# Cross-attention with layer norm: score matmuls of 32 x 128 split into tiles of 32 x 64

## The chip, the cores and the metric

The kernel runs on one core of a Trainium2 chip. The core has a matrix engine (TensorE, PE in the profile, with its weight loads shown as PEld), a vector engine (VectorE, DVE), an activation engine (ScalarE, ACT), a general engine (GpSimd, POOL) and a queue that issues most DMAs (SyncE, SP). The metric is the device time of one execution in microseconds (us). The kernel before took 534.93 us, the median of three runs (534.4 to 535.43).

## The reference

Cross-attention of 4 x 2048 query rows on 4 x 77 context rows, 512 columns, 16 heads of 32 columns, then a residual and a layer norm, in float32:

```python
qs  = (q @ wq).reshape(4, 2048, 16, 32).transpose(0, 2, 1, 3)
ks_ = (k @ wk).reshape(4, 77, 16, 32).transpose(0, 2, 1, 3)
vs  = (v @ wv).reshape(4, 77, 16, 32).transpose(0, 2, 1, 3)
scores = einsum('bhqd,bhkd->bhqk', qs, ks_) / sqrt(32)
scores = where(mask, -inf, scores)
attn = einsum('bhqk,bhkd->bhqd', softmax(scores), vs)
out = attn.transpose(0, 2, 1, 3).reshape(4, 2048, 512) @ wo + q
out = (out - mean(out)) / sqrt(var(out) + 1e-5) * gamma + beta
```

Here `q` is `x`, and `k` and `v` are both the context. The change touches only the product of `qs` and `ks_`.

## The kernel before, in words

**Tiles.** The 8192 query rows are 64 tiles t of 128 rows; 16 tiles belong to one batch and share its 77 keys, its values and its mask. Two tiles make a pair. Heads come in four groups g of four (j = 0 to 3): head 4g + j has its 32 columns in partitions 32j to 32j + 31 of the transposed query projection `q` (512 rows wide, `qd` in the code) and of the transposed keys `kct`.

**Work of one tile, by engine.**
- `q_visit` (matmuls L160, 12 for 512 query rows and one m): query projection on PE from split operands (`xth`, `xtl`, `wqh`, `wql`); DVE copies it out (`q_evac`, L177).
- `scores` (L273 to L290, matmul L283): for each g and j one matmul. The loaded operand is `q` for one head (32 partitions, 128 query rows as columns), the streamed operand is `kct` (32 partitions, 77 keys), the result is 128 x 77 in a PSUM bank. Bank `sc[j]` holds the four heads of one j side by side. So a matmul uses 32 of the array's 128 rows and all 128 columns, and four of them, with j = 0 to 3, use four different row groups and write four different banks.
- `maxima` (L297, DVE): per head, adds the mask, moves the scores to SBUF (`pbuf`) and takes the row's maximum (`nm`).
- `exps` (L311, ACT): per head exponential and row sum. `recip` (L322, DVE) and `normalise` (L327, POOL) divide.
- `transp` (L351, DVE) transposes in blocks of 32, and `regroup` (DMAs L363, 12 a pair, on SP) sorts the blocks into `PT`.
- `av` (matmul L381, in the very last tiles `av_tile`, L396): attention times values for a pair. The loaded operand has 96 partitions and 32 columns; four heads use four column groups side by side. ACT and DVE take the result out in two halves (`AH` L412, `AL` L416).
- `o_proj` (matmul L445, 12 a tile): output projection from `AH`, `AL`, `woh`, `wol`. In the end some tiles also get their residual through PE (`resid`, L434). Then `residual` (L454) and the moments on DVE, the scaling on ACT, gamma and beta on POOL, and the store.

**Order.** Every engine runs its instructions in the order in which the code issues them. All PSUM results share eight banks in turn (`bank`, eight buffers), so a matmul group waits until the bank that it gets has been read. The first 54 tiles (27 pairs, `CUT`) are issued by a loop; in its regular part PE's order for a pair u, u + 1 is scores(u), o_proj(u - 6), one q_visit, scores(u + 1), av of the pair two before, o_proj(u - 5), one q_visit. Once in a batch DVE also builds the next batch's mask (`mask_bias` L264 and L265, `mask_nan` L269 to L271), in two consecutive pairs. The last ten tiles are issued from the text `ORDER`, in which an `S54` is scores(54), and so on. Before the loop come the loads, the splitting of the weights, the keys and the first query projections.

Of the kernel before, what the change touches and what calls it, by code (L numbers as in the profile page):

```python
# [17 lines left out]
P = 128  # L18
D = 512
H = 16  # L20
HD = 32
NK = 77
# [4 lines left out]
GH = 4  # L27
# [40 lines left out]
def xattn_layernorm(  # L68
# [15 lines left out]
    nc = tc.nc  # L84
    NB = mask.shape[0]
    TPB = mask.shape[2]
# [8 lines left out]
    def bank(name):  # L95
        return ps.tile([P, 512], F32, tag="mm", name=name)
# [8 lines left out]
    kct = const.tile([P, NG, NB, NK2], F32, name="kct")  # L105
# [28 lines left out]
    def keys_of(h):  # L134
        return slice(TAIL_K, NK2) if h % 2 == 0 else slice(0, NK)
# [137 lines left out]

    def scores(t):
        qs = qd[t // 4]
        rs = slice((t % 4) * P, (t % 4) * P + P)
        nmax[t] = sb.tile([P, H], F32, tag="nm", bufs=3, name=f"nm_{t}")
        sums[t] = sb.tile([P, H], F32, tag="sum", bufs=3, name=f"sum_{t}")
        sc = scs[t] = [bank(f"sc_{t}_{j}") for j in range(GH)]
        for g in range(NG):  # L280
            for j in range(GH):
                q = slice(HD * j, HD * (j + 1))
                nc.tensor.matmul(  # L283
                    sc[j][:, g * NK : (g + 1) * NK],
                    qs[q, g, rs],
                    kct[q, g, t // TPB, keys_of(j)],
                    start=True,
                    stop=True,
                )

    def maxima(t, lo, hi):
        pb = pbuf[t % NPB]
# [242 lines left out]
    for c in range(NC_D):  # L535
        split(x0h[:, c], x0l[:, c], f0[c // 2 * 2][:, 0, c % 2])
        split(wqh[:, c], wql[:, c], stage_a[:, 0, c])
        for m in range(NG):
            for n, (w, r) in enumerate(((wqh, x0h), (wqh, x0l), (wql, x0h))):
# [4 lines left out]
                    start=(c == 0 and n == 0),  # L544
                    stop=(c == NC_D - 1 and n == 2),
# [37 lines left out]
    for u in range(0, 2 * CUT, 2):  # L583
# [6 lines left out]
        for t in (u - 4, u - 3):  # L590
            if t >= 0:
                load_x(t)
        scores(u)
        maxima(u, 0, H // 2)
        for q in evac:
# [45 lines left out]
        if k == TPB - 2 and m + 1 < NB:  # L641
            mask_nan(m + 1)

        scores(u + 1)
        maxima(u + 1, 0, 3 * H // 4)
        recip(u)
# [42 lines left out]

    tile_ops = {  # L690
        "S": scores, "r": recip, "n": normalise, "t": transp, "W": av_tile, "x": load_x, "X": resid, "O": o_proj,
        "+": residual, "u": rsqrt_one, "y": centre, "z": finish, "k": scale, "f": affine, "w": store,
    }
# [81 lines left out]
```

## Time and profile before

| | us |
|---|---|
| Time, median of three runs | 534.93 |
| The profiled execution: span of its instructions | 533.1 |
| PE busy | 522.3 (98%) |
| PE weight loads busy (beside PE) | 399.1 (75%) |
| DVE busy | 486.2 (91%) |
| ACT busy | 459.6 (86%) |
| POOL busy | 400.7 (75%) |
| L283 score matmuls, 2048 instructions, busy on PE | 72.5 |

The profiled execution has its own span, 533.1 us from the first to the last instruction; the runs' times are taken separately and hold a little more than that span. How to read the views: in the **timeline** a row is a start, a length, the engine, line, operation and tile, and a count (x32: 32 instructions merged); the length runs to the end of the last. A row of the **windows** is a stretch in us, its length, then busy us and count for each engine, the clock that PE was granted, the busy share of the DMA engines and GB/s. A row of a **line's instructions** is a count, then shortest, median and longest duration in ns and the first and last start. A row of the **groups by line** has busy us and mean ns of one, then the idle time before them and what ended it. The **chain that ended last** goes back from the last instruction to what released each step. Matmul ends are modelled: a matmul's duration holds its way through the array, so several overlap, and the rate is read from starts.

### The profile page before, as it was taken

What the parts mean: (1) busy time and instruction counts of PE and PEld (TensorE: products, weight loads), DVE (VectorE), ACT (ScalarE), POOL (GpSimd) and SP (SyncE); (2) the same over time, 40 slices, a digit from 0 to 9 for tenths busy, and PEclk for the clock granted to TensorE, in tenths of its full rate; (3) what the DMA queues carried; (4) which work ended last, traced back from release to release, by engine and by line L of the source; (5) the groups of instructions that cost most, each with busy time, mean ns of one, the idle gap of its engine ahead of it and who ended that gap; (6) DMA issues with size and microseconds to landing.
All of it is one profiled execution on the core that took longest, in us unless ns stands there. A gap on an engine that the chain in (4) does not pass through costs nothing.

```text
span 533.1 us, 16107 instructions
## 1 busy us (share of the span) xinstructions
PE 522.3 (98%) x4810; PEld 399.1 (75%) x4810; DVE 486.2 (91%) x2592; ACT 459.6 (86%) x2215; POOL 400.7 (75%) x363
## 2 busy tenths in 40 slices
PE   8999999999999999999999999999999999999994
PEld 6977777777777777777777777777777777776672
DVE  5689989999998889889998998889999989999897
ACT  6687799999899999998899999998899999998600
POOL 0626547998798988887899888888799888665751
PEclk9999999999999999999999999999999999999997
DMA  8934667788677887787677787867687775849744
GB/s 300 402 120 111 202 173 195 222 232 226 176 187 213 227 215 208 208 226 201 179 213 214 208 221 217 232 165 211 191 216 216 219 191 159 219 129 281 226 138 157
DMA packets 58695, 109.96 MB, mean 206 GB/s; under 512 B 9392, under 2 KB 11056, under 8 KB 58608
## 3 DMA queue, kind: packets, MB, share of 16 engines
q1 hardware_dynamic: 55424, 102.64, 68.6%
q0 software_dynamic: 2304, 5.24, 3.5%
q10 hardware_dynamic: 880, 1.05, 0.7%
q8 instruction: 38, 0.62, 0.5%
q14 instruction: 49, 0.40, 0.2%
HBM read 41.79 MB, written 16.78 MB: 110 GB/s over the span
## 4 chain that ended last, share of the span: by engine, by line
PE 88%; DMA 5%; DVE 4%; issue 1%; SPq 1%; ACT 0%; DVEq 0%
PE pq L160 32%; PE po L445 30%; PE sc L283 12%; PE pa L381 9%; DMA PT<-B 2%; PE pv L221 2%; DMA out<-o 2%; PE pk L186 1%; DVE B L351 1%; DVE pbuf L297 1%; DMA stage_a<-wq 1%; PE pq L540 1%; DVE o_end L504 1%; DVE o_end L501 1%; SPq L363 0%
## 5 line engine op out<-in xcount | busy, mean ns | idle before, releaser
L311 ACT ACTIVATE pbuf<-pbuf,nm 128x77 f32<-128x77 f32 x1024 | 352.9, 352 | 31.4 <-DVE nm L297 26.5
L311 ACT ACTIVATION_READ_ACCUMULATOR pbuf<-pbuf,nm 128x1 f32 x1024 | 197.3, 193 | 0.0
L327 POOL TENSOR_TENSOR pbuf<-pbuf,ri 128x1232 f32<-128x1232 f32 x63 | 142.9, 2268 | 61.1 <-DVE ri L322 47.4
L297 DVE CUSTOM_DVE_ANT_0 pbuf<-sc,mb 128x77 f32<-128x77 f32 x1024 | 169.0, 231 | 4.9 <-PE sc L283 3.3
L445 PE MATMUL po<-woh,AH 128*128 128x512 f32 x256 | 108.6, 424 | 0.0
L445 PE MATMUL po<-wol,AH 128*128 128x512 f32 x256 | 100.4, 392 | 0.0
L445 PE MATMUL po<-woh,AL 128*128 128x512 f32 x256 | 100.1, 391 | 0.0
L160 PE MATMUL pq<-xth,wqh 128*128 128x512 f32 (+1 forms) x256 | 98.4, 385 | 0.0
L160 PE MATMUL pq<-xtl,wqh 128*128 128x512 f32 (+1 forms) x256 | 97.9, 382 | 0.0
L160 PE MATMUL pq<-xth,wql 128*128 128x512 f32 (+1 forms) x256 | 97.8, 382 | 0.0
L351 DVE STREAM_TRANSPOSE B<-pbuf 128x1280 f32<-128x1280 f32 x64 | 95.5, 1493 | 1.9 <-POOL pbuf L327 1.8
L297 DVE DVE_READ_ACCUMULATOR2_ANT nm<- 128x1 f32 x1024 | 84.0, 82 | 0.0
L283 PEld LDWEIGHTS sc<-kct,q 32*128 32x128 f32 x2048 | 63.0, 186 | 22.6 <-issue 12.0
L283 PE MATMUL sc<-kct,q 32*128 32x77 f32 x2048 | 72.5, 277 | 0.0
L153 POOL TENSOR_TENSOR xtl<-xtf,xth 128x1024 fp32r<-128x1024 f32 x28 | 67.1, 2397 | 1.9 <-ACT xth L149 1.9
L482 POOL TENSOR_TENSOR o<-o,bet 128x512 f32<-128x512 f32 x48 | 63.1, 1314 | 3.8
L445 PEld LDWEIGHTS po<-woh,AH 128*128 128x128 f32 x256 | 48.0, 187 | 23.1 <-DVE nm L297 6.6
L481 POOL TENSOR_TENSOR o<-o,gam 128x512 f32<-128x512 f32 x48 | 61.6, 1284 | 0.2
L381 PE MATMUL pa<-PT,vsb 96*32 96x256 f32 x992 | 60.0, 382 | 1.6 <-DMA out<-o 0.9
L445 PEld LDWEIGHTS po<-woh,AL 128*128 128x128 f32 x256 | 48.1, 188 | 10.7
L160 PEld LDWEIGHTS pq<-xth,wqh 128*128 128x128 f32 x256 | 48.1, 188 | 10.2 <-DVE nm L297 0.4
L445 PEld LDWEIGHTS po<-wol,AH 128*128 128x128 f32 x256 | 48.1, 188 | 9.6 <-issue 1.4
(106 smaller groups left out, 664.4 us busy)
## 6 DMA issues: line engine op xcount, KB each, us to landing
PT<-B SPq DMA_DIRECT2D x346, 128.0 KB, 2.4
xtf<-xT SPq DMA_DIRECT2D x28, 512.0 KB, 4.8
o<-x SPq DMA_DIRECT2D x56, 256.0 KB, 4.9
out<-o SPq DMA_DIRECT2D x56, 256.0 KB, 2.9
PT<-B POOLq DMA_DIRECT2D x21, 128.0 KB, 5.2
o_end<-x SPq DMA_DIRECT2D x8, 256.0 KB, 5.4
out<-o_end SPq DMA_DIRECT2D x8, 256.0 KB, 2.4
xtf<-xT SPq DMA_DIRECT2D x4, 256.0 KB, 5.0
```

What stands on the lines that cost most here:

```text
L153: nc.gpsimd.tensor_tensor(l, fx.pop((g, c)), h.bitcast(F32), ALU.subtract)
L160: nc.tensor.matmul(pq, w[:, c, m * P : (m + 1) * P], r[:, c, rs], start=(n == 0), stop=(n == 11))
L221: nc.tensor.matmul(pv[:NK2, :], ctx_s[c][i][:, b, :], v[c], start=(n == 0), stop=(n == 11))
L283: nc.tensor.matmul(sc[j][:, g * NK : (g + 1) * NK], qs[q, g, rs], kct[q, g, t // TPB, keys_of(j)], start=True, stop=True,)
L297: nc.vector.tensor_tensor_reduce(pb[:, h // 2, (h % 2) * NK : (h % 2 + 1) * NK], scs[t][j][:, g * NK : (g + 1) * NK], mb[:, t % TPB, keys_ ...
L311: nc.scalar.activation(pb[:, h // 2, (h % 2) * NK : (h % 2 + 1) * NK], pb[:, h // 2, (h % 2) * NK : (h % 2 + 1) * NK], AF.Exp, bias=nmax[t ...
L327: nc.gpsimd.tensor_tensor(pv, pv, rv.to_broadcast((P, NP, 2, NK)), ALU.mult)
L351: nc.vector.transpose(bt.rearrange("p c q r -> p q c r"), pbuf[t % NPB].rearrange("p q (c r) -> p q c r", c=5),)
L381: nc.tensor.matmul(pas[b, g // 2][HD * j : HD * (j + 1), (g % 2) * BLK : (g % 2 + 1) * BLK], vsb[:, 2 * b // TPB, HD * h : HD * (h + 1)], ...
L445: nc.tensor.matmul(pos[t], a[:, c, rs], w[:, c, :], start=(first and c == 0 and n == 0), stop=(c == NC_D - 1 and n == 2),)
L481: nc.gpsimd.tensor_tensor(o, o, gam, ALU.mult)
L482: nc.gpsimd.tensor_tensor(o, o, bet, ALU.add)
```

## The change: what it does

`scores` issues two matmuls where it issued one: the first for query rows 0 to 63 of the tile, the second for rows 64 to 127. Each loads 32 partitions x 64 columns of `q` and streams the same 77 columns of `kct`; the results go to partitions 0 to 63 and 64 to 127 of the same bank and columns as before. In the array the second half takes columns 64 to 127, so that with four row groups eight tiles of 32 x 64 lie side by side. The order is: for each g first the four j of the first half, then the four j of the second. All that reads the scores is unchanged.

```diff
     def scores(t):
         qs = qd[t // 4]
-        rs = slice((t % 4) * P, (t % 4) * P + P)
...
         for g in range(NG):
-            for j in range(GH):
-                q = slice(HD * j, HD * (j + 1))
-                nc.tensor.matmul(
-                    sc[j][:, g * NK : (g + 1) * NK],
-                    qs[q, g, rs],
-                    kct[q, g, t // TPB, keys_of(j)],
-                    start=True,
-                    stop=True,
-                )
+            for half in range(0, P, P // 2):
+                for j in range(GH):
+                    q = slice(HD * j, HD * (j + 1))
+                    r0 = (t % 4) * P + half
+                    nc.tensor.matmul(
+                        sc[j][half : half + P // 2, g * NK : (g + 1) * NK],
+                        qs[q, g, r0 : r0 + P // 2],
+                        kct[q, g, t // TPB, keys_of(j)],
+                        start=True,
+                        stop=True,
+                    )
```

## The prediction

> **What bounds the kernel now.** I read the page first (busy shares, then the chain that ended last), then the windows by stage, and last the timeline of TensorE (PE) around single stages.
>
> ```profile
> PE 522.3 (98%) x4810; PEld 399.1 (75%) x4810; DVE 486.2 (91%) x2592; ACT 459.6 (86%) x2215; POOL 400.7 (75%) x363
> PE 88%; DMA 5%; DVE 4%; issue 1%; SPq 1%; ACT 0%; DVEq 0%
> PE pq L160 32%; PE po L445 30%; PE sc L283 12%; PE pa L381 9%; DMA PT<-B 2%; PE pv L221 2%; DMA out<-o 2%; PE pk L186 1%; DVE B L351 1%; DVE pbuf L297 1%; DMA stage_a<-wq 1%; PE pq L540 1%; DVE o_end L504 1%; DVE o_end L501 1%; SPq L363 0%
> L454 DVE TENSOR_TENSOR o<-po,o 128x512 f32<-128x512 f32 x53 | 36.3, 686 | 17.2 <-PE po L445 17.1
> ```
>
> PE is the bound: 98% busy, 88% of the last chain, and the longest wait of VectorE (DVE) is for PE, 17.1 us at the residual. The score stage, L283, is 12% of the chain. How near are the others? The windows hold busy us and instruction counts of PE, PE's weight loads (PEld), DVE, ScalarE (ACT) and GpSimd (POOL).
>
> ```profile
> 20.00:80.02 60.02, 60.02 (x543) 46.71 (x541) 52.51 (x308) 48.75 (x249) 30.66 (x16) 1.00 0.61 179
> 80.02:202.64 122.62, 122.62 (x1154) 94.06 (x1153) 114.89 (x631) 118.05 (x571) 106.43 (x89) 1.00 0.78 210
> 202.64:325.25 122.61, 122.61 (x1154) 94.05 (x1153) 112.95 (x630) 115.12 (x553) 105.77 (x88) 1.00 0.77 208
> 325.25:432.57 107.32, 107.32 (x1010) 82.30 (x1009) 99.43 (x552) 100.60 (x484) 92.61 (x77) 1.00 0.77 209
> 432.57:490.00 57.43, 57.43 (x606) 42.17 (x606) 56.65 (x361) 52.29 (x282) 41.14 (x43) 1.00 0.69 187
> ```
>
> From 20 to 432.57 us PE has no idle time. That is the regular loop (two query tiles, one pair, in 122.61/8 = 15.33 us). ACT is close behind (115.12 of 122.61 in eight pairs), DVE next (112.95). From 432.57 on, in the hand-ordered end, DVE is busy 56.65 of 57.43 us.
>
> **The change part by part.** It replaces 16 matmuls of a tile by 32 of half the columns. First, what one stage consists of.
>
> ```profile
> 202.32 0.39 PE L160 MATMUL pq<-xth,wql 128*128 128x512 f32 x1
> 202.64 1.13 PE L283 MATMUL sc<-kct,q 32*128 32x77 f32 x32
> 203.70 0.50 PE L445 MATMUL po<-woh,AH 128*128 128x512 f32 x1
> ...
> 202.63 0.98 PEld L283 LDWEIGHTS sc<-kct,q 32*128 32x128 f32 x32 [0.35 <-issue]
> ...
> 202.63:202.66 0.03, 0.02 (x4) 0.03 (x4) 1.00 0.40 68
> 202.66:202.74 0.08, 0.08 (x4) 0.08 (x4) 1.00 1.32 282
> 202.74:202.80 0.06, 0.06 (x4) 0.06 (x8) 1.00 0.64 137
> ...
> L283 PEld LDWEIGHTS sc<-kct,q x2048: 181/187/187, 22.1 to 485.0; 32*128 32x128 f32 x187
> L283 PE MATMUL sc<-kct,q x2048: 270/270/330, 22.1 to 485.0; 32*128 32x77 f32 x187
> ...
> 202.71 1.06 PE sc L283 x32
> ```
>
> 64 tiles x 16 matmuls are 1024, the profile has 2048: an f32 matmul is two instructions (two passes), each with its own load. The windows show four loads and four matmuls started together, then nothing, then the next four loads: rounds of four, one per group of 32 rows, eight rounds a stage. The length of a round, from the block of 1.13 us: 1.13 less the last matmul's 0.27, less the 0.06 by which the first is longer (330 against 270 ns), less 0.02 for the spread of four, over 7 = 0.111 us. The loads, 0.98 less 0.187 less 0.02 over 7, give 0.110: the next four come when the previous four are through. A stage takes 1.06 us to the next stage's first matmul: 0.86 of rounds and 0.20 of emptying the array.
>
> What sets the 0.111? The attention matmuls (pa) have four column groups side by side, with short loads:
>
> ```profile
> 210.40 1.93 PE L381 MATMUL pa<-PT,vsb 96*32 96x256 f32 x32
> ...
> 515.90 1.96 PE L396 MATMUL pa<-PT,vsb 96*32 96x128 f32 x64
> ...
> L381 PEld LDWEIGHTS pa<-PT,vsb x992: 106/110/110, 59.7 to 503.4; 96*32 96x32 f32 x199
> L381 PE MATMUL pa<-PT,vsb x992: 376/379/403, 59.7 to 503.6; 96*32 96x256 f32 x199
> ...
> L396 PE MATMUL pa<-PT,vsb x64: 272/273/297, 515.9 to 517.6; 96*32 96x128 f32 x64
> ...
> 210.40 0.42 PE L381 MATMUL pa<-PT,vsb 96*32 96x256 f32 x4
> ...
> 210.40 0.14 PEld L381 LDWEIGHTS pa<-PT,vsb 96*32 96x32 f32 x5
> ```
>
> By the same reckoning a round with 256 moving columns is (1.93 - 0.379 - 0.024 - 0.02)/7 = 0.215 us, one with 128 is (1.96 - 0.273 - 0.024 - 0.02)/15 = 0.1095: 0.83 ns a column, so 77 columns would need 0.067 us. The score round takes 0.111, so its 128-column load is what it waits for, not the 77 columns that stream.
>
> After the change a load has 64 columns. Estimate of its time: half of 0.111 is 0.056; by the two load durations (187 ns for 128 columns, 110 for 32: 0.80 ns a column) it is 0.111 - 64 x 0.8 = 0.060. Issuing: four matmuls with their loads start within 0.42 - 0.403 = 0.02 us, 6 to 7 ns each, so eight take 0.053. All of it lies under the 0.067 of streaming. **If the eight tiles run at once**, a round has eight matmuls and lasts 0.067, and a stage still has eight rounds. Its length: 0.04 for the longer first matmul (between the 24 ns of pa and the 60 of sc), 7 x 0.067 = 0.47, 7 x 0.0067 = 0.05 for the spread, 0.20 of emptying: 0.76 us against 1.06. **0.30 us saved a stage.** The bounds of the unknown part: a round no shorter than the 0.053 of issue (0.40 saved), no longer than two turns of 0.067 (0.18 lost; below).
>
> Nothing else moves: the same order on every engine, the same four banks, no DMA, no new wait, since only the last matmul of a bank is waited for and the second half's first writes come behind the first half's on the same engine. PE issues 128 instructions a stage where it issued 64; the 0.053 above is their price, and it stays hidden as long as streaming is longer.
>
> How much reaches the end? The stages S0 to S53 lie ahead of 432.57, where PE is without a gap: 54 x 0.30 = 16.2 us. Of the last ten I count nothing:
>
> ```profile
> 454.43 8.17 PE pq L160 x36
> 466.65 1.42 DVE B L351
> 469.46 3.86 DMA out<-o
> 474.04 1.42 DVE B L351
> ```
>
> there the chain passes to DVE and its transposes, and DVE is full in the window. What is late next in the loop: eight pairs would take 122.61 - 16 x 0.30 = 117.8 us. ACT needs 115.12 in one window, but 118.05 in the first, so 0.3 is lost there. And ACT is made to wait, in two bursts a batch, when DVE does the mask work:
>
> ```profile
> L311 ACT ACTIVATE pbuf<-pbuf,nm 128x77 f32<-128x77 f32 x256 | 88.3, 354 | 7.5 <-DVE nm L297 7.5
> ```
>
> These 7.5 us are its whole slack in eight pairs; 2.7 would be left, so it catches up more slowly, the AH copies come later, and the output projection may wait for them. I take 0.4 us for each of three batches, and 1.2 us of ACT and DVE still late when the end begins, where DVE cannot make it up. Both are judged, between nothing and half of the gain. Sum: 16.2 - 0.3 - 1.2 - 1.2 = 13.5 us. The profiled span is 533.1, so 519.6; the median of the runs, 534.93, stands 1.8 above that span, so **521.4 us**.
>
> A rule of the Trainium skill speaks against the change: "TensorE: Matmul & The Clock Gate", The mechanism, says that a weight load overlaps matmuls in flight only where they use another row group. The two halves share their row group. By it a round would be a load and a matmul one after the other. The trace disagrees as far as it goes: in the row at 210.40 five loads lie in 0.14 us, the fifth beside four matmuls of 0.4 us on the same 96 rows. The same page measured 16 tiles of 32 by 32 at 10.6 times one tile's rate; no run here shows rows and columns split at once.
>
> **The rivals.**
>
> (1) The halves take turns (slower). In this trace row groups run side by side (sc) and column groups do (pa), never both. If the two halves of a row group stream in turn, a round is 2 x 0.067 = 0.134 against 0.111: 8 x 0.023 = 0.18 us a stage, and as PE is the bound all of 54 stages count: +9.9, **544.8**; with all 64, 546.7. It decides once a round passes 0.111, that is when less than 0.023 of 0.067 overlaps. Against it: four column groups take their own streams from the same rows at full rate in pa.
>
> (2) Loads wait for the matmuls of their row group (slower): a round of 0.060 + 0.067 = 0.127, +0.13 a stage, 54 stages: +6.9, **541.8**. The page named above states this. The 210.40 row speaks against it.
>
> (3) Matmuls start strictly in the code's order, so that the second pass of the first half holds up the second half: a group of heads then takes 2 x (0.067 + 4 x 0.0067) = 0.188 instead of 2 x 0.111, 4 x 0.034 = 0.14 a stage, 54 stages: -7.3, **527.6**. Against it: now four first passes start within 0.03 us, with their second passes later, so a pass that waits doesn't hold up other tiles.
>
> (4) No gain: the loads of the two halves share one path, 2 x 0.056 = 0.111 a round as now, **534.9**. The five overlapping pa loads speak against it.
>
> **How the numbers follow.** Forecast 0.62, (1) 0.13, (2) 0.05, (3) 0.13, (4) 0.07. The forecast's own range: all 64 stages at 0.30 give 534.9 - 19.2 = 515.7; with half of the gain lost between the engines, 526. To hold 8 in 10 the range must also take in (3) and (4): 515.5 to 536.0, which leaves out (1) and (2), 0.18. A measurement of this kernel tells about 0.2% (1.07 us) from no change. Faster: the forecast and (3), 0.75. Same: (4), 0.07. Slower: (1) and (2), 0.18.
>
> **What would show it.** L283 in the timeline: 64 matmuls of 32x77 in a block of about 0.83 us (0.56 to the last start and 0.27), eight starting together; 1.1 or less than 0.6 would refute the round of 0.067. The next stage 0.76 us after the first score matmul. The pair at 14.7 us in the windows, PE still without idle time; if ACT or DVE is full there and PE waits at L445, the loss between engines is larger than I took. The end, from S54 on, as long as before, about 100 us. It is wrong if rounds are longer than 0.111, or if the shorter stage only adds idle time before L445.

## The result and the profile after

The changed kernel takes **533.93 us** (median of 20 runs, 532.62 to 536.01); before, measured beside it, 535.12 (20 runs). The ratio is 0.9979, 95% interval 0.9970 to 0.9989: about 1.2 us faster, where 13.5 were forecast. The profiled span is 531.8 us, before 533.1.

The page of the changed kernel, busy times, chain and groups (most line numbers have moved by one):

```profile
PE 514.6 (97%) x6858; PEld 393.0 (74%) x6858; DVE 485.3 (91%) x2592; ACT 459.4 (86%) x2215; POOL 401.1 (75%) x363
PE 29%; ACT 28%; DVE 26%; DMA 9%; issue 3%; SPq 3%; POOL 1%; DVEq 0%; ACTq 0%
L382 PE MATMUL pa<-PT,vsb 96*32 96x256 f32 x992 | 60.2, 381 | 7.5 <-DMA o<-x 1.9
L284 PE MATMUL sc<-kct,q 32*64 32x77 f32 x4096 | 62.5, 238 | 0.4 <-DVE vsb L228 0.4
```

The same group of pa in the page of before:

```profile
L381 PE MATMUL pa<-PT,vsb 96*32 96x256 f32 x992 | 60.0, 382 | 1.6 <-DMA out<-o 0.9
```

PE is 7.7 us less busy, but the span is only 1.3 shorter. Ahead of pa there are now 7.5 us of idle time, where there were 1.6. With such gaps on PE the chain no longer stays on it: from 88% it falls to 29%. That does not make ACT and DVE the bound, as the windows of the same eight pairs show:

```profile
80.83:202.75 121.92, 120.27 (x1666) 92.61 (x1665) 114.43 (x631) 118.04 (x571) 106.51 (x89) 1.00 0.80 212
202.75:324.62 121.87, 120.25 (x1665) 92.63 (x1664) 112.55 (x630) 114.90 (x553) 105.92 (x88) 1.00 0.79 209
431.33:490.00 58.67, 57.45 (x930) 41.94 (x930) 57.66 (x361) 54.18 (x291) 41.83 (x45) 1.00 0.72 189
```

Eight pairs take 121.9 us against 122.6, and PE is idle for 1.6 of them, 0.2 a pair; in the end DVE is full, as before. Where is PE idle? The timeline of PE around an even and an odd score stage, and the same odd stage in the row of pa's instructions (PEldq: what PE's sequencer does ahead of a load), of the changed kernel:

```profile
202.75 0.95 PE L284 MATMUL sc<-kct,q 32*64 32x77 f32 x64
203.63 0.50 PE L446 MATMUL po<-woh,AH 128*128 128x512 f32 x1
...
209.27 0.95 PE L284 MATMUL sc<-kct,q 32*64 32x77 f32 x64
210.40 0.85 PE L382 MATMUL pa<-PT,vsb 96*32 96x256 f32 x12 [0.18 <-PE sc L284]
...
L382 PEldq EVENT_SEMAPHORE  x6: 51/51/51, 209.9 to 210.6; - x6
```

and the odd stage before:

```profile
209.34 1.13 PE L283 MATMUL sc<-kct,q 32*128 32x77 f32 x32
210.40 0.85 PE L381 MATMUL pa<-PT,vsb 96*32 96x256 f32 x12
...
L381 PEldq EVENT_SEMAPHORE  x4: 51/51/51, 209.6 to 210.0; - x4
```

The even stage has become 0.18 us shorter, 0.88 from its first matmul to po's. The odd one has become 0.07 longer, 1.13 to pa's. In the odd stage the sequencer takes pa's waits (eight DMA queues, DVE and PE, in five instructions ahead of the first load) one every 0.106 us. Before, there was no wait for PE among them, and the four instructions had been taken by 210.0, under the score matmuls; now the first comes at 209.9, and pa's load starts at 210.37, behind the fifth.

Inside a stage the timeline of its first part, matmuls and loads, shows what was forecast and what was not:

```profile
202.75 0.54 PE L284 MATMUL sc<-kct,q 32*64 32x77 f32 x33
...
202.75 0.39 PEld L284 LDWEIGHTS sc<-kct,q 32*64 32x64 f32 x33 [0.35 <-issue]
```

33 matmuls start within 0.54 - 0.22 = 0.32 us (the last one's own length taken off), in rounds of eight, which from the second on are 0.067 us apart: in the single instructions they begin at 202.865, .931, .998. That is the forecast round. The other 31 need 0.41: after the 33rd load, 0.253 us into the stage, one comes at 0.319 and the next at 0.374, and from there a whole f32 matmul (two loads, two passes) comes every 16.7 ns. The last starts 0.726 us after the first, not 0.557.

A pair's two stages thus give 0.18 - 0.07 = 0.11 us where 0.61 (twice 0.304) was forecast, and the pair takes 15.24 us (431.33 - 80.83 over 23) against 15.33.

### The profile page after: what moved, and what is told of

It is laid out like the page before. It is cut to its first block, busy times and chain, and to the rows that moved or that the text cites. A ratio compares the mean times of both kernels' runs of the same rounds, so it can differ in the third digit from the quotient of the medians.

```text
span 531.8 us, 20432 instructions
## 1 busy us (share of the span) xinstructions
PE 514.6 (97%) x6858; PEld 393.0 (74%) x6858; DVE 485.3 (91%) x2592; ACT 459.4 (86%) x2215; POOL 401.1 (75%) x363
## 4 chain that ended last, share of the span: by engine, by line
PE 29%; ACT 28%; DVE 26%; DMA 9%; issue 3%; SPq 3%; POOL 1%; DVEq 0%; ACTq 0%
ACT pbuf L312 23%; PE po L446 10%; PE pq L160 9%; DVE pbuf L298 7%; DVE B L352 5%; DMA PT<-B 4%; PE pa L382 3%; PE sc L284 3%; DVE q L177 3%; DMA o<-x 3%; ACT AH L413 3%; SPq L364 2%; DVE st L460 2%; ACT o L478 2%; PE pk L186 1%
## 5 line engine op out<-in xcount | busy, mean ns | idle before, releaser
L312 ACT ACTIVATION_READ_ACCUMULATOR pbuf<-pbuf,nm 128x1 f32 x1024 | 201.4, 197 | 0.0
L284 PEld LDWEIGHTS sc<-kct,q 32*64 32x64 f32 x4096 | 51.9, 130 | 23.6 <-issue 16.5
L284 PE MATMUL sc<-kct,q 32*64 32x77 f32 x4096 | 62.5, 238 | 0.4 <-DVE vsb L228 0.4
```

The lines of the kernel that those rows point to most:

```text
L284: nc.tensor.matmul(sc[j][half : half + P // 2, g * NK : (g + 1) * NK], qs[q, g, r0 : r0 + P // 2], kct[q, g, t // TPB, keys_of(j)], start= ...
L312: nc.scalar.activation(pb[:, h // 2, (h % 2) * NK : (h % 2 + 1) * NK], pb[:, h // 2, (h % 2) * NK : (h % 2 + 1) * NK], AF.Exp, bias=nmax[t ...
```

## The experiments

Two theories were set against each other; the recorded texts call them A and B, and later a rival stands against A alone. **Theory A**: PE's instructions come too late. Some 33 loads with their matmuls are ready when a stage begins, the rest come slower than the array takes them; and as the sequencer is no longer ahead, pa's waits stand in PE's way. **Rival B**: the shorter stage can't be used, since ACT and DVE don't follow.

**Even or odd stages alone.** One line is put into `scores`, and `P // 2` becomes `w` in the three places below it; for the odd ones it reads `== 1`:

```diff
-            for half in range(0, P, P // 2):
+            w = P // 2 if t % 2 == 0 else P
+            for half in range(0, P, w):
```

> Splits only the even tiles (in the loop those followed by the output projection); odd tiles keep whole matmuls. Theory A (PE's instruction supply: 64 places are filled ahead, what comes after arrives later at 17 ns a matmul, and the waits of the attention matmuls behind an odd tile are no longer taken ahead of time): even stages 0.88 us, odd stages 1.06, a pair 15.33 - 0.18 = 15.15 us, 27 pairs give -4.9, with up to 1 lost at start and end 530 to 531. Rival B (ACT and DVE cannot follow a faster PE): no better than the full split, 533.5 to 534.5.

> Splits only the odd tiles (in the loop those followed by the attention matmuls). Theory A: odd stage 1.13 us against 1.06, a pair +0.07, in all +2, 536 to 537.5, slower than before. Rival B: between before and the full split, 534 to 535.

Measured: even 531.69 us, ratio 0.9941 (0.9928 to 0.9954); odd 536.01, ratio 1.0021 (1.0010 to 1.0032). The first is 0.7 above what A said (S54 comes 4.1 us sooner than before, the end 3.4). Even stages again last 0.88. The second lies in A's range, but not by A's sum, which had the odd stage at 1.13 us. In the odd stages of this kernel,

```profile
210.17 0.95 PE L285 MATMUL sc<-kct,q 32*64 32x77 f32 x64
211.20 1.93 PE L383 MATMUL pa<-PT,vsb 96*32 96x256 f32 x32
...
L383 PEldq EVENT_SEMAPHORE  x4: 51/51/51, 210.8 to 211.1; - x4
```

the block of matmuls is the short one, 0.95, but pa comes 1.03 us after the start: next to nothing is won. Only four waiting instructions stand ahead of pa here (210.8 to 211.1), hence 1.03 and not 1.13: the fifth belongs to the split of the even stages, and the kernel with even stages alone has five too. The pair takes 15.32 us, as before, so that the time agrees with A is luck; its profile (of the slowest of twelve runs) loses 0.9 us ahead of S8 and 2.5 behind S54, and why is open. The even split alone beats the change. Of B nothing is left for the even stages, where the 0.18 us a pair arrive in full (pair 15.15).

**Room on PE.** Three of the twelve output matmuls of every odd tile in the loop are left out of the kernel before, so that its output lacks their products:

```diff
             for n, (a, w) in enumerate(((ah, woh), (ah, wol), (al, woh))):
+                if n == 1 and c > 0 and tt and t < 2 * CUT:
+                    continue
```

> The kernel before, with 3 of the 12 output projection matmuls left out in each odd tile of the loop (three of the four products with the low part of wo), so that PE has 0.68 us a pair less to do and nothing else changes. Theory A: the others follow, 27 x 0.68 = 18 less a loss of 0 to 4: 517 to 521. Rival B: they don't, 531 or more.

Measured: 524.25 us, ratio 0.9799 (0.9786 to 0.9811), between the two. Its chain and eight pairs:

```profile
ACT 55%; DVE 23%; DMA 8%; issue 4%; SPq 4%; PE 4%; POOL 0%; DVEq 0%; ACTq 0%
...
197.26:315.09 117.83, 117.58 (x1129) 89.83 (x1128) 112.48 (x631) 114.77 (x554) 106.33 (x89) 1.00 0.81 219
```

The pair takes 14.7 us, as forecast for the change: the other engines follow in the loop, and S54 is reached 14.75 us sooner (417.82 against 432.57). At the end of the span 11.0 are left: 3.8 us are lost behind S54, where ACT is full at first,

```profile
417.82:437.82 20.00, 19.00 (x221) 14.22 (x220) 19.42 (x127) 20.00 (x104) 17.70 (x17) 1.00 0.73 198
```

busy 20.00 of 20 us. That ACT makes the loss is argued from this and from its 55% of the chain, and not shown: in a kernel below (528.35 us) ACT is as full in the first 20 us behind S54, and the end there is no longer than before (100.4 us against 100.6). So B holds at most for a loss of some 4 us of 15, and the change lost its gain before that.

**Waits early, by a small matmul.** In the changed kernel, ahead of the projection that stands before the odd stage:

```diff
+        if ahead is not None:
+            nc.tensor.matmul(pq[:, :4], vsb[:, 2 * ahead // TPB, 0:P],
+                             pts[ahead][:NK2, :, 0, 0:1], start=True, stop=True)
...
```

`ahead` is the pair that pa will work on; the lines that hand it on are not shown. The control has the same matmul and splits the even stages alone.

> All stages split as in the change, and one small matmul more per pair (96 rows of PT by 128 columns of vsb, 4 moving columns), put ahead of the projection that stands before the odd score stage: it takes the eight DMA waits of pa there, while PE is still at the output projection. In the trace of the change the odd score stage lasted 1.134 us to pa's first matmul, 0.408 of it after the last score matmul, with five waiting instructions 0.106 us apart. Theory A (these waits are no longer taken ahead and stand in PE's way): one is left, the odd stage falls to about 0.88 to 0.92 us, 0.22 to 0.25 us saved in each of some 25 pairs, less some 0.04 a pair for the small matmul: 528.4 to 530. Rival (the gap belongs to the change from tiles of 64 columns to pa's of 32, or to the late instructions themselves): the odd stage stays at 1.1 us, 534 to 535.

> Control for the small matmul: only the even tiles are split (531.69 us without it), and pa's DMA waits are taken early in the same way. Theory A: behind an unsplit stage the waits were already hidden, so nothing is gained, and the small matmul costs 0 to 0.05 us a pair: 531.7 to 533. Rival (the waits cost something behind an unsplit stage too): the odd stage falls below 1.061 us and the time below 531.

Measured: 542.12 us, ratio 1.0138 (1.0111 to 1.0164), and 541.48, 1.0130 (1.0101 to 1.0159). Both totals missed, though the odd stage of the first did what A said:

```profile
211.97 0.28 PE L169 MATMUL pq<-PT,vsb 96*128 96x4 f32 x2
212.12 0.48 PE L160 MATMUL pq<-xth,wqh 128*128 128x512 f32 x1
212.43 0.39 PE L160 MATMUL pq<-xtl,wqh 128*128 128x512 f32 x1
...
215.02 0.95 PE L292 MATMUL sc<-kct,q 32*64 32x77 f32 x64
215.90 1.93 PE L390 MATMUL pa<-PT,vsb 96*32 96x256 f32 x32
...
L169 PEldq EVENT_SEMAPHORE  x101: 51/51/3233, 52.7 to 426.4; - x101
  issue: 8.4, 10
```

0.88 us from the scores to pa. But the small matmul costs: it takes the place of the projection's first, and the second, at 212.43, comes 0.46 us later, where two follow each other in 0.23. So 0.23 us a pair are lost, which eats the gain. And its waits came too early: one lasts 3.2 us, and ahead of the small matmul or its load there were ten gaps of 8.4 us in all (of the matmuls alone, eight gaps and 5.3 us). The control has such costs too (six gaps, 5.7 us) and no gain: its odd stage stays 1.061 us.

**Half of the heads split.** `w = P // 2 if g < 2 else P`, and the mirror image `g >= 2`:

> In every stage only the first two of the four groups of heads are split (four rounds of eight, then four rounds of four): 96 instructions a stage instead of 128. Theory A (64 instructions are ready at the start, and one that is taken is followed by a new one only 0.375 us later): the 64 split ones start in 0.27 us, the others from 0.375 on in rounds of 0.111: 0.71 us from the first start to the last, even stages about 0.90 us, odd ones about 1.10 as pa's waits come late: 531.5 to 533. Rival (no queue, the array alone sets the rounds): 4 x 0.067 + 3 x 0.111 + 0.02 = 0.62 us from first start to last.

> The mirror image: only the last two groups of heads are split, the same 96 instructions. Theory A: the first four rounds of four take 32 instructions in 0.445 us, and their followers come 0.375 us after each, so the last of the stage start near 0.82 us, later than with the first half split; even stages about 0.98 to 1.0 us, odd ones 1.2 to 1.3: 535 to 539, slower than the first half split by 3 us or more. Rival (instructions are supplied at a steady rate, or the array alone sets the rounds): 4 x 0.111 + 3 x 0.067 + 0.05 = 0.69 us from first start to last, and the time within 1 us of the other half.

Measured: 536.29 us, ratio 1.0025 (1.0015 to 1.0035), and 541.78, 1.0125 (1.0103 to 1.0148). Both times lie above what A said; that splitting the second half is slower by 5.5 us (A: by 3 or more) fits it. From first to last start it is 0.867 and 0.912 us: neither theory. Where the tile shape changes within the stage, the array empties: 0.155 us from the last start of the split matmuls to the first of the whole ones, 0.200 in the other direction. That eats the gain and hides what the pair of kernels was to tell. Of pa's waits it tells something: with whole matmuls last the odd stage ends as the even one, 1.07; with split ones last, pa comes 0.19 us later,

```profile
212.25 1.14 PE L285 MATMUL sc<-kct,q 32*128 32x77 f32 x48
213.51 0.85 PE L383 MATMUL pa<-PT,vsb 96*32 96x256 f32 x12
```

1.26 us after the start.

**Waits early, without a matmul.** The changed kernel, with a dependency of the projection's last matmul ahead of the odd stage on PT's transfers; then the same with the odd split and the dependency only from the ninth tile on; then a control with even stages split alone. In the code `mm` is that last matmul and `regs[ahead]` holds the transfers:

```diff
+            for d in regs[ahead] if ahead is not None else ():
+                tc.add_manual_dep(mm.ins, d.ins.name, SYNC, reason="ahead of pa")
...
```

> All stages split as in the change, and pa's eight DMA waits put on the last matmul of the projection ahead of the odd score stage (a dependency, no added matmul). With the small matmul the odd stage had fallen to 0.882 us as theory A said, but the small matmul cost 0.23 us a pair and seven of 22 pairs stood still for about 0.9 us, where its waits came too early. Theory A: the odd stage again 0.88 us and the usual pair 15.24 - 0.25 = 14.98 us; if these pairs no longer stand still, 25 x 0.25 = 6 us less than the change: 527 to 529. Rival (PT lands too late for any earlier wait): the odd stage 0.88 us too, but pairs of 16 us remain: 532 to 538.

> The same, but the odd stages are split, and the waits moved, only from the ninth tile on: in the change the first eight tiles had lost 0.8 us against before, with even stages split alone 0.06. Theory A: 0.5 to 1.5 us less than the run beside it: 526 to 528. Rival: as there, 532 to 538, less the same.

> Control: only the even tiles are split (531.69 us), and pa's DMA waits lie on the last matmul of the projection (528.35 us with all stages split). Theory A: behind an unsplit odd stage the waits were hidden already, the odd stage stays 1.061 us, the pair 15.15: 531 to 532.5. Rival (the early waits help by themselves): 530 or less.

Measured: **528.35 us**, ratio 0.9873 (0.9858 to 0.9887); 528.92, 0.9884 (0.9868 to 0.9901); the control 532.79, 0.9962 (0.9949 to 0.9976). The odd stage of the first:

```profile
208.00 0.95 PE L288 MATMUL sc<-kct,q 32*64 32x77 f32 x64
208.88 1.93 PE L386 MATMUL pa<-PT,vsb 96*32 96x256 f32 x32
...
L386 PEldq EVENT_SEMAPHORE  x2: 51/51/51, 208.6 to 208.9; - x2
```

0.88 us, one waiting instruction instead of five ahead of the load, the usual pair 14.99. In the control the odd stage stays 1.061 and nothing is gained; it comes out 0.3 us above what A said, as one pair, from S8 to S10, takes 15.95 instead of 15.15. In the kernel of 528.35 us that pair takes 16.06. So the early waits are worth something only where the stage has become too short to hide them, and taking them out of PE's way gives 5.6 us (533.93 to 528.35). This version beats both kernels. The late start brought nothing (0.57 us more, not less): that the odd split of the first tiles costs the 0.8 us which the change is late at S8 was wrong. One profile can't tell such a cost at all: the kernel before, which runs unchanged in the two kernels of the next experiment up to its end, reaches S8 there at 79.38 and 81.55 us (80.02 in its own profile), and needs 352.55 us from S8 to S54 all three times. So the pairs behind S8 compare far more closely than the time to S8 does, and whether the change costs anything there stays open.

**The pace of the instructions by itself.** Behind the end of the kernel before, runs of score matmuls without a wait among them, into banks that nobody reads (the numbers are tiles and columns of the array; the code of `probe` is not shown):

```diff
+    probe(8, P, F32); probe(8, P // 2, F32); probe(8, P // 4, F32)
+    probe(8, P, BF16); probe(8, P // 2, BF16)
```

> The kernel before, and at its end, on PE alone, five runs of eight tiles of score matmuls into banks that nobody reads: f32 of 128, 64 and 32 columns, then bf16 of 128 and 64. Its time is longer by these; only the runs are read. Whole f32: 0.89 us a tile. Split f32 without a pause between the tiles: if the supply is a rate of 17 ns a matmul, 32 x 17 = 0.54 us a tile and 64 x 17 = 1.07 with 32 columns; if it is 64 places that come back 0.37 us after a start, 128 x 0.37 / 64 = 0.74 and 1.48; if nothing but streaming counts, 0.54 and 0.54.

and, with 64 columns of the array each (here the second number is the moving columns), `probe(4, 77, F32)`, `probe(4, 8, F32)`, `probe(8, 8, BF16)`, `probe(8, 77, BF16)`:

> The kernel before, with four more runs of split score matmuls behind its end, without any wait inside a run: f32 with 77 and with 8 moving columns, bf16 with 8 and with 77. With 8 columns the array has next to nothing to do. Theory A (instructions come late): the 8-column matmuls show the same picture as the 77-column ones, some 33 matmuls and their loads at 7 to 8 ns each, then a gap, then groups of 33 or so every 0.30 to 0.38 us, 9 to 11.5 ns a matmul. Rival (the array: the second pass on a tile holds up what follows): the 8-column matmuls start one after the other at about 6.7 ns without a gap, 0.43 us for 64, and only the 77-column ones show gaps.

The first took 589.0 us and the second 557.58; their totals tell nothing, their timelines do. Of the first, loads, then matmuls:

```profile
534.02 0.39 PEld L743 LDWEIGHTS probe<-kct,q 32*64 32x64 f32 x33 [0.81 <-issue]
...
534.02 1.67 PE L743 MATMUL probe<-kct,q 32*64 32x77 f32 x128 [0.65 <-issue]
537.75 2.14 PE L743 MATMUL probe<-kct,q 32*64 32x77 f32 x128 [2.06 <-issue]
```

and of the second, the matmuls and the windows of the same stretches (after the counts: the granted clock):

```profile
526.88 2.46 PE L743 MATMUL probe<-kct,q 32*64 32x77 f32 x200
...
543.44 1.23 PE L743 MATMUL probe<-pbuf 32*64 32x8 bf16 x128 [1.92 <-issue]
...
550.35 1.40 PE L743 MATMUL probe<-pbuf 32*64 32x77 bf16 x128 [1.12 <-issue]
...
526.88:529.20 2.32, 2.32 (x201) 2.30 (x200) 2.29 (x6) 0.00 (x0) 1.71 (x4) 1.00 0.62 229
...
543.44:544.67 1.23, 1.23 (x128) 1.15 (x128) 0.00 (x0) 0.00 (x0) 0.00 (x0) 0.50 0.05 13
550.35:551.75 1.40, 1.40 (x128) 1.26 (x128) 0.00 (x0) 0.00 (x0) 0.00 (x0) 0.50 0.06 12
```

The whole tiles of the first kernel run in the old rounds of 0.111, 0.89 us a tile, as expected. The split ones show the picture of the change with no wait in sight: 33 loads at once, then a pause, then whole f32 matmuls 16.7 ns apart, in groups of 34 loads every 0.376 us. Of the three sums on record for it that comes nearest to the one of 64 places that come back 0.37 us after a start. 200 of them start within 2.46 - 0.22 us, 11.2 ns each, 0.72 us for a stage's 64; the array, in rounds of eight, needs 0.067/8 = 8.4.

With bf16, one load and one pass a matmul, the late ones come singly, 8.3 ns apart, with 77 columns and with 8 alike; what the array holds up starts in bunches of eight instead. A matmul with a tenth of the streaming comes no faster: against the rival. In the second and third rounds of that run eight matmuls with their loads start every 54 ns, so array and loads could go faster than the 66 ns in which eight late ones come. And two instructions in 8.3 ns at a granted clock of 0.50 are the pace of the four in 16.7 ns at 1.00: it doesn't go with the array's clock. But with 8 columns there are no further pauses after the first one, which A had expected; with 77 there is one of some 0.03 us after every 33 loads. So the first 33 go at the array's pace and the late ones at that of the instructions' coming, two every 8.3 ns; what makes the pauses, and keeps f32 at 11 ns, is not settled. A run without loads was not tried. The granted clock, 0.50 for the bf16 rows, was the same for the f32 run with 8 columns and for the tiles of 32 columns, which were slower than the 8.3 ns throughout and tell nothing here.

## Why the prediction was wrong

- *What bounds the kernel: PE.* Right: time taken off PE in the loop reached S54 nearly in full (even split 0.18 us a pair; room on PE 0.61 of 0.68).
- *The eight tiles run at once, a round lasts 0.067.* Right for the first half of a stage. Rivals (1), (2) and (3) fall with it. The rule of the Trainium skill ("TensorE: Matmul & The Clock Gate", The mechanism) that a load overlaps matmuls in flight only on other row groups does not hold here: 33 loads lie within 0.39 us beside matmuls of all four row groups. Rival (4) came near the time, by another mechanism than its own. So 533.93 lies in the forecast's range by luck: its upper end, 536.0, was set there to take in (3) and (4), and the forecast's own range ended at 526.
- *"PE issues 128 instructions a stage where it issued 64; the 0.053 above is their price, and it stays hidden."* **This step failed.** The 6 to 7 ns were read off a short run, four matmuls that were ready. A stage's 64 loads and matmuls don't all stand ready; the later ones start at 11 ns. From first to last start it is 0.726 us and not 0.557: 0.17 of the 0.30 lost in each stage. The Trainium skill, on the same page ("TensorE: Matmul & The Clock Gate", Architectural detail), states that TensorE's queue holds 64 instructions. The trace agrees with it roughly, as 33 loads with their matmuls are 66, but whether the queue or what fills it makes the pause isn't shown here.
- *"Nothing else moves ... no new wait."* **This step failed too.** Four waiting instructions of pa had always stood behind the score stage, hidden by it, and the split of the even stages added a fifth. With the score instructions late (the first of the waits comes 0.60 us into the odd stage, where it came at 0.30) they stand open: 1.134 - 0.881 = 0.25 us in each odd stage. The dependency on the projection took just that away.
- *0.20 of emptying.* It became 0.155 where nothing else waits: 0.045 better than forecast.
- The sum for a pair: forecast 0.61; less 2 x 0.17 and 0.25, plus 2 x 0.045, gives 0.11. The pair fell by 0.09.
- *Coupling, 2.7 of 16.2 us.* It was put too small: with 14.75 us reaching S54, 3.8 were lost behind it. For this change it hardly counted: S54 came 1.24 us sooner, the end 1.3. *The end as long as before*: right, 100.5 us against 100.6.

Of the list of signs, the length to the last start (0.73 against 0.56), the next stage after 0.76 us (0.88 and 1.13), the pair (15.24 against 14.7) and the PE without idle time failed. Neither of the two ways in which it called itself wrong came true: rounds did not pass 0.111, and the idle time lies ahead of pa and not of L445.

## What to carry to other kernels

Smaller matmuls side by side shorten a stage only as long as their instructions are ready: count loads and passes of the stage, take the pace from a run in a trace that is longer than the 66 instructions which went at once here, and not from the first few. A stage that becomes shorter or busier in instructions also uncovers the waits of what follows it; look at the sequencer's waiting instructions behind it, and put their waits on an earlier, long matmul that already stands there, no earlier than needed. Halves of a change tried alone show quickly which half pays for the other.

## What the runs showed of the hardware

- 33 loads with their matmuls start at the array's pace, then there is a pause, and the rest come two instructions every 8.3 ns, in groups of 34 loads with their matmuls every 0.376 us for f32. The pace of two every 8.3 ns was the same at a granted clock of 1.00 (f32) and 0.50 (bf16).
- A waiting instruction of PE's sequencer took 0.106 us where it lay open.
- A change of the tile shape between score matmuls cost 0.155 us (64 to 128 columns) or 0.200 (128 to 64). The end of a stage shows the same two figures where nothing else waits: 0.155 us from the last start of a 64-column tile to what follows it (0.881 - 0.726), 0.200 from that of a 128-column one (1.061 - 0.861).
- In the bare probe PE went through the first 328 (first kernel) or 200 matmuls (second) without a stop, and from there on stood still after every 128 loads and 128 matmuls, for 0.65 and 2.06 us in the rows above. The Trainium skill, "Runtime: NRT & Kernel Launch", Instruction fetch mechanics, has instructions fetched in blocks of 256 and the fetch mostly hidden. The count agrees with the stops of the probe; the hiding doesn't in straight code this dense, if the stops are the fetch, which no run here shows. The kernel itself, with 64 score matmuls a stage and longer ones between, showed no such stop in the stages read here.
